# A selective-scan layer on one Trainium2 core: the residual sum put on TensorE, two more scan buffers, and a second pair of every tile multiplied by C on GpSimd

## The chip, the cores and the metric

The kernel runs on one core of one Trainium2 chip. The metric is the device time of one execution in microseconds; the figure of a kernel is the median of its runs. Besides, one execution was taken by the hardware profiler; all views of the profile below come from that one execution, and its own time differs a little from the median.

## What is computed

The program is a stack of four layers on an input x of shape (8, 384, 32, 32), in float32: eight samples, 384 channels, 1024 positions. Each layer normalises x by groups of channels, transforms it and adds the result to x. Layers 0 and 2 are selective state-space ("Mamba") layers, layer 1 is a deformable convolution, layer 3 a displaced depthwise filter. The change touches layer 0 alone. Cut to what matters, layer 0 is:

```python
xz = xseq @ in_proj_w.T                       # 384 -> 2 x 768
xin, z = jnp.split(xz, 2, axis=-1)
u = silu(causal_conv3(xin) + conv_b)
dbc = u @ x_proj_w.T                          # 768 -> 24 + 16 + 16
dt, Bm, Cm = split(dbc)
dt = softplus(dt @ dt_proj_w.T + dt_proj_b)   # per channel and token
def step(h, inp):                             # h: 768 channels x 16 states
    dA = jnp.exp(dt_t[..., None] * A)
    h = dA * h + (dt_t * u_t)[..., None] * B_t[:, None, :]
    y = jnp.einsum('bdn,bn->bd', h, C_t)
    return (h, y)
y = ys + u * D
y = y * silu(z)
x = x + y @ out_proj_w.T                      # the layer's residual sum
```

## The kernel before

**Tiling.** A sample's 1024 tokens are cut into two halves of 512, called steps here: 16 steps in layer 0, a first half (`h == 0`) and a second half (`h == 1`) for each sample. The 768 inner channels are six tiles of 128 partitions (`j`, 0 to 5). The 16 states are taken two at a time, so that each tile has eight pairs (`m`, 0 to 7). One pair of one tile of one step is a unit: 48 units in a step, 768 in layer 0. A unit's data are 128 x 1024 numbers (two states, 512 tokens each).

**A unit** goes through five engines:
- ScalarE (ACT): `decays` (L437) makes exp(dt A) in PSUM, two instructions. There are two such PSUM buffers (`da`).
- GpSimd (POOL): `inputs` (L442) makes the product with B in `db` (three buffers).
- VectorE (DVE): `scan` (L452) runs the recurrence. Normally it writes over `da`.
- Then the states are multiplied by C (`with_c`): normally on VectorE (L466), from `da` into an `hs` buffer in SBUF, 128 x 1024. For the pairs that the table `GP_C` names, the scan writes an `hs` buffer itself and GpSimd multiplies it in place (L463)[...]. There are four `hs` buffers (L450, L465), handed out in the order of the units.
- TensorE (PE): `read_out` (L473 to L486) adds the two states' columns of `hs` into the PSUM tile `y` by products with the identity (L483); the first read of a tile is preceded by the product of u with the diagonal of D (L479).

When all eight pairs of a tile are read, `close` (L503, VectorE) multiplies `y` with the gate and writes it into `u`. There is one `y` buffer, so the next tile's first product (L479) comes after this close.

**Who multiplies with C in layer 0.** `GP_C[0]` holds, by half and by whether the tile's number is even or odd, the pairs for GpSimd: pairs 0 and 4 in every tile of first halves and in even tiles of second halves, pair 0 alone in odd tiles of second halves.

**The order of the work.** Every engine executes its instructions in the order in which the loop at L704 emits them; the order is written out by hand (`manual_schedule`). In unit t of a step (t = 8 j + m) the loop emits: the reads that are due "early"; the ScalarE items planned for t; the scan and, on VectorE, its `with_c`; the decays of the unit two ahead; the VectorE items for t; the GpSimd product with B for the unit three ahead and, where it is GpSimd's, `with_c`; the GpSimd items; the PE items; and the reads that are due "late". A pair that VectorE multiplied is read late, one unit after its own (the last pair of a tile early in the unit after), a pair of GpSimd's early, three units after its own (L744, L745).

**What is planned beside the scans** (`plan`, L591 to L661). A step carries along the end of the step before it and the front of the step after it. The items that matter here, for layer 0:
- `close` of tile j - 1 in unit 8 j + 1, so the close of tile 1 is in unit 17.
- Of the step before: `residual` (L506) in unit 9 reloads x from DRAM into a two-buffer ring; `out_proj` (L516) for the three output groups o on PE in units 8 and 9, 10 and 11, 12 and 13; `out_take` (L536) on VectorE in units 10, 12 and 14, which adds the PSUM result to x in place and, after the third, stores x with one DMA.
- Of this step: `z_proj` (L492, for tile 1 in unit 9), `dt_proj` (L389, for tile 3 in unit 14), and on ScalarE `soft_exp` (L395 to L398, from unit 15).
- Of the step after: `inner` (L333) on PE in units 15, 16, 17, 24, 25 and 26, followed on ScalarE by `conv_last` (L337) and on VectorE by `conv` (L353) one and two units later; `x_proj` (L369) in units 30 and 31. If it is a first half, the group statistics also fall in units 0 to 8.

After the last unit (L748 to L760) the last step's close, residual load, `out_proj` and `out_take` run alone, and then the next layer begins.

All float32 products on TensorE appear in the profile as two matmul instructions each.

Of the kernel before, what the change touches and what calls it, by code (L numbers as in the profile page):

```python
# [8 lines left out]
F32 = mybir.dt.float32  # L9
AF = mybir.ActivationFunctionType  # L10
ALU = mybir.AluOpType
# [4 lines left out]
P = 128  # L16
# [6 lines left out]
ND = DI // P  # L23
# [3 lines left out]
TS = L // 2  # L27
W_MID = 1536


GP_C = {0: (((0, 4), (0, 4)), ((0, 4), (0,))), 2: (((0,), (0,)), ((0,), (0,)))}
GP_ADD = {0: (), 2: (1, 2, 3, 5, 6)}
ENGINES = {mybir.EngineType.Activation, mybir.EngineType.PE, mybir.EngineType.DVE, mybir.EngineType.Pool}
FF = 4 * C
# [57 lines left out]
class Net:  # L92
# [107 lines left out]
    def ssm_layer(self, li, src, dst, shift=None):  # L200
        tc, nc, ins = self.tc, self.nc, self.ins
        mlp = li == 2
        gp_c, gp_add = GP_C[li], GP_ADD[li]
        with ExitStack() as ctx:
            wp = ctx.enter_context(tc.tile_pool(name=f"w{li}", bufs=1))
            p1 = ctx.enter_context(tc.tile_pool(name=f"p1_{li}", bufs=1))
            p2 = ctx.enter_context(tc.tile_pool(name=f"p2_{li}", bufs=2))
# [5 lines left out]
            for h in (1, 0):  # L213
                x = p2.tile([P, G, TS], F32, name="x", tag="x")
# [44 lines left out]
            def w_mid(src, k):  # L259
                t = p2.tile([P, k, W_MID // k], F32, name="wm", tag="wm", bufs=3)  # L260
                n = src.shape[2]
                nc.sync.dma_start(out=t[:, :, :n], in_=src)
                return t
# [180 lines left out]
            def scan(s, j, m):  # L444
                if j == 0 and m == 0 and s["h"] == 0:
                    s["sib"]["st"] = p2.tile([P, ND, NS], F32, name="st")
                da, db = s["da", m], s["db", m]
                h = da
                if m in gp_c[s["h"]][j % 2]:
                    h = s["hs", m] = p2.tile([P, 2, TS], F32, name="hs", tag="hs", bufs=4)  # L450
                h1, da1, db1 = (t.rearrange("p i l -> p (i l)") for t in (h, da, db))
                nc.vector.tensor_tensor_scan(h1, da1, db1, 0.0, ALU.mult, ALU.add)  # L452
                s["h", m] = h
# [6 lines left out]
            def with_c(s, j, m):  # L460
                c = s["bc"][m][:, 1]
                if m in gp_c[s["h"]][j % 2]:
                    nc.gpsimd.tensor_tensor(s["hs", m], s["hs", m], c, ALU.mult)  # L463
                else:
                    hs = s["hs", m] = p2.tile([P, 2, TS], F32, name="hs", tag="hs", bufs=4)  # L465
                    nc.vector.tensor_tensor(hs, s["da", m], c, ALU.mult)  # L466

            def add_pair(s, j, m):
# [41 lines left out]
            def out_proj(s, o, k0, k1):  # L510
                if k0 == 0:
                    wo = w_mid(wout_d[:, :, o * P : (o + 1) * P], ND) if mlp else wout[:, :, o * P : (o + 1) * P]
                    s["out", o] = self.psum("ps_o"), wo
                ps, wo = s["out", o]
                for k in range(k0, k1):
                    nc.tensor.matmul(ps, wo[:, k, :P], s["u"][:, k, :], start=(k == 0), stop=(k == ND - 1))  # L516

            def store(s, o):
                if mlp:
# [9 lines left out]
            def out_take(s, o):  # L529
                if mlp:  # L530
                    if o == 0:
                        s["t"] = p2.tile([P, G, TS], F32, name="t", tag="xn", bufs=3)
                    nc.scalar.copy(s["t"][:, o, :], s["out", o][0])
                else:
                    xo = s["x"][:, o, :]
                    nc.vector.tensor_tensor(xo, xo, s["out", o][0], ALU.add)  # L536
                    store(s, o)

            def mlp_up(s, q, f):
# [51 lines left out]
            def plan(prev, s, nxt):  # L591
                act, dve, pool, pe = queues = [[[] for _ in range(T + NU)] for _ in range(4)]

                def put(q, t, fn, *args):
                    if not args or args[0]:
                        q[t].append((fn, *args))

                for j in range(ND):
                    t = NU * j
                    put(dve, t + 1, close, *((s, j - 1) if j else (prev, ND - 1)))  # L600
                    put(pe, (0, 9, 18, 27, 33, 41)[j], z_proj, s, j)
                    g = (3, 11, 20, 29, 35, 44)[j]
                    put(act, g, gate, s, j)
                    if j in (2, 3):
                        put(act, g, silu, nxt, 3 * (j - 2), 3 * (j - 1))
                    put(act, g, exp_ln)

                    n, k = (s, j + 2) if j + 2 < ND else (nxt, j + 2 - ND)
                    put(pe, t + 6, dt_proj, n, k)
                    put(act, t + 7, soft_exp, n, k)  # L610
                    put(dve, t + 8, soft_rest, n, k)
                    put(act, t + 9, soft_ln, n, k)
                    put(pool, t + 10, soft_sum, n, k)
                put(pe, 0, norm_load, nxt)
                if nxt and nxt["h"] == 0:
                    put(dve, 2, norm_stats, nxt, 0)
                    put(dve, 3, norm_stats, nxt, 1)
                    put(dve, 3, lambda n: n.update(gn_mv=self.gn_aggr(n["gn_st"])), nxt)
                    put(pe, 4, lambda n: n.update(gn_ps=self.gn_mean(n["gn_mv"])), nxt)
                    put(dve, 5, lambda n: n.update(gn_grp=self.gn_dev(n["gn_mv"], n["gn_ps"])), nxt)  # L620
                    put(act, 6, lambda n: n.update(gn_dm=self.gn_square(n["gn_grp"][1])), nxt)
                    put(pe, 6, lambda n: n.update(gn_ps=self.gn_mean2(n["gn_dm"])), nxt)
                    put(dve, 7, lambda n: n.update(gn_var=self.gn_sum(n["gn_grp"][0], n["gn_ps"])), nxt)
                    put(act, 8, lambda n: n.update(gn=self.gn_rstd(n["gn_grp"][0], n["gn_var"])), nxt)
                    put(act, 8, lambda n: n["sib"].update(gn=n["gn"]), nxt)
                put(act, 9, norm_apply, nxt)
                if mlp:
                    put(pe, 10, ln_mean, nxt)
                    put(dve, 11, ln_center, nxt)
                    put(act, 12, ln_square, nxt)  # L630
                    put(pe, 12, ln_var, nxt)
                    put(act, 13, ln_rstd, nxt)
                    put(dve, 13, ln_scale, nxt)
                    put(act, 14, ln_affine, nxt)
                for d, t in enumerate((15, 16, 17, 24, 25, 26)):
                    put(pe, t, inner, nxt, d)
                    put(act, t + 1, conv_last, nxt, d)
                    put(dve, t + 2, conv, nxt, d)
                put(pe, 30, x_proj, nxt, 0, ND // 2)
                put(pe, 31, x_proj, nxt, ND // 2, ND)  # L640
                put(act, 32, x_store, nxt)
                for m in range(NU):
                    put(pool, 41 + m, load_bc, nxt, m)
                put(act, 7 if mlp else 9, residual, prev)
                for o, (t, e) in enumerate(((1, 2), (3, 4), (5, 6)) if mlp else ((8, 9), (10, 11), (12, 13))):
                    put(pe, t, out_proj, prev, o, 0, ND // 2)
                    put(pe, e, out_proj, prev, o, ND // 2, ND)
                    put(act if mlp else dve, e + (1 if mlp else 2), out_take, prev, o)
                if mlp:
                    ups = ((7, 8, 11, 13), (22, 23, 28, 29), (37, 38, 39, 40))  # L650
                    downs = ((19, 20, 21), (34, 35, 36), (43, 44, 45))
                    for q, g in enumerate((17, 33, 42)):
                        for f, t in enumerate(ups[q]):
                            put(pe, t, mlp_up, prev, q, f)
                            put(act, t + 1, up_take, prev, q, f)
                        put(act, g, gelu, prev)
                        put(act, g, exp_ln)
                        for o, t in enumerate(downs[q]):
                            put(pe, t, mlp_down, prev, q, o)
                            put(dve, t + 2, down_take, prev, q, o)  # L660
                return queues  # L661
# [6 lines left out]
            with tc.manual_schedule(engines=ENGINES):  # L668
                s = steps[0]
# [34 lines left out]
                for i, (s, j, m) in enumerate(units):  # L704
                    c, t = divmod(i, T)
                    if t == 0:
# [6 lines left out]
                        act, dve, pool, pe = queues  # L713
# [6 lines left out]
                    if not mine:  # L720
                        with_c(s, j, m)
# [14 lines left out]
                    if mine:  # L736
                        with_c(s, j, m)
# [6 lines left out]
                    k = 3 if mine else 2 if m in gp_add else 1  # L744
# [12 lines left out]
                    stats = list(range(last))  # L757
                for o in range(G):
                    out_proj(s, o, 0, ND)
                    out_take(s, o)  # L760
                if mlp:
                    kernels_a()
# [1084 lines left out]
```

## Time and profile before

| what | value |
|---|---|
| median of three runs | 9474.54 us (9471.22 to 9475.02) |
| the profiled execution's own time | 9480.32 us |
| its span, first to last instruction | 9478.5 us |
| mean granted TensorE clock | 0.948 |
| busy share of the span | PE 90%, DVE 86%, ACT 68%, POOL 61% |
| closes of layer 0 (L503, 96 of them) | start at 97.5 us to 3022.4 us |
| L452, scans of the whole program | 2912.7 + 602.4 us on DVE |
| L442, products with B | 3611.1 us on POOL |
| L483, reads with the identity | 2605.0 us on PE |

How to read it. Times are counted from the first instruction. "PE" are matmuls, "PEld" the loads of their stationary operand, which overlap with them. The matmuls' ends are modelled, so a matmul of 592 ns by the profile may be followed by the next one before it ends; the distance from start to start tells the rate. A busy share of the whole span mixes four layers; layer 0 takes about the first third, and only its stretches matter here. In the tables by windows, each row is a stretch "from:to" with its length, and then the busy time of each engine in it with the number of its instructions, the granted clock, and the DMA share. In the tables of waits, a row is "engine line waited for whom: total us, times, longest us". In timelines, "[1.22 <-PE y L483]" says that the engine sat idle for 1.22 us before this instruction and that the PE's instruction of L483 ended the wait.

### The profile page before, as it was taken

The page shows a single profiled execution, that of the slowest core. Times are in us where ns is not written, and L with a number is a line of the kernel's source. Part 1 is how long each engine was busy: PE and PEld are TensorE (multiplying, and loading weights), DVE is VectorE, ACT ScalarE, POOL GpSimd, SP SyncE. Part 2 cuts the span into 40 slices and gives each one's busy share as a digit, 9 for nine tenths or more (in the row PEclk, how much of TensorE's full clock was granted, in tenths as well). Part 3 has the DMA queues.
Part 4 walks back from the last instruction along what each step waited for, and adds up shares of the span by engine and source line. Part 5 has one row for each costly group of instructions (what it writes and reads, how often), then busy time and mean ns, then how long its engine had stood idle before and what let it go on. Part 6 is the DMA issues. An engine that isn't in the chain of part 4 may idle for free. (4 is left out here: it accounts for less than half of the span.)

```text
span 9478.5 us, 87409 instructions
## 1 busy us (share of the span) xinstructions
PE 8496.4 (90%) x27916; PEld 4511.6 (48%) x27916; DVE 8121.2 (86%) x8881; ACT 6479.3 (68%) x10147; POOL 5774.0 (61%) x3801
## 2 busy tenths in 40 slices
PE   7898888889887899999999997699999999999987
PEld 3333333333333677677777776244343443434333
DVE  7999999999997678778778777899999999999973
ACT  6666666666664677778778777667777777777750
POOL 7888888888887000000000000899999999999974
PEclk8999999999998999999999998799999999999998
DMA  2111211121111233333333333233232433333336
GB/s 92 68 56 46 85 53 53 50 85 56 49 68 51 77 80 88 90 83 84 93 79 88 89 83 87 92 100 95 91 94 87 121 112 96 93 91 90 120 102 127
DMA packets 566065, 791.98 MB, mean 84 GB/s; under 512 B 244243, under 2 KB 397235, under 8 KB 542041
## 3 DMA queue, kind: packets, MB, share of 16 engines
q1 hardware_dynamic: 503492, 775.85, 27.9%
q10 hardware_dynamic: 62100, 10.44, 0.7%
q8 instruction: 223, 3.65, 0.2%
q14 instruction: 250, 2.04, 0.1%
HBM read 716.49 MB, written 69.66 MB: 83 GB/s over the span
## 5 line engine op out<-in xcount | busy, mean ns | idle before, releaser
L442 POOL TENSOR_TENSOR db<-du,bc 128x1024 f32<-128x1024 f32 x1536 | 3611.1, 2356 | 419.0 <-DVE hs L452 230.7
L452 DVE TENSOR_TENSOR_SCAN da<-da,db 128x1024 f32<-128x1024 f32 x1272 | 2912.7, 2290 | 199.4 <-ACT da L437 145.4
L483 PE MATMUL y<-hs,ident 128*128 128x512 f32 x5184 | 2605.0, 638 | 376.2 <-DVE hs L466 233.8
L437 ACT ACTIVATE da<-dt,na 128x512 f32<-128x512 f32 x3072 | 2120.0, 691 | 911.1 <-DVE hs L466 679.9
L410 POOL TENSOR_TENSOR dt<-dt,sp_e 128x512 f32<-128x512 f32 x192 | 244.2, 1272 | 2932.1 <-DVE sp_e L402 2932.1
L483 PEld LDWEIGHTS y<-hs,ident 128*128 128x128 f32 x5184 | 1018.0, 203 | 1863.2 <-issue 1125.3
L1515 PE MATMUL wacc<-fsm,fxk 128*128 128x221 f32 (+34 forms) x10624 | 1657.1, 315 | 98.1 <-DVE fsm L1485 95.5
L1515 PEld LDWEIGHTS wacc<-fsm,fxk 128*128 128x128 f32 x10624 | 1570.1, 195 | 236.5 <-DVE fsm L1485 159.5
L466 DVE TENSOR_TENSOR hs<-da,bc 128x1024 f32<-128x1024 f32 x1272 | 1557.7, 1225 | 115.5 <-PE y L483 12.1
L1485 DVE TENSOR_TENSOR fsm<-fhy,fhx 128x170 f32<-128x170 f32 (+42 forms) x3216 | 1170.8, 428 | 346.2 <-PE wacc L1515 319.3
L1445 ACT ACTIVATE fhy<-fpyx,cell 128x416 f32<-128x416 f32 (+9 forms) x1280 | 645.5, 576 | 388.7 <-DVE fsm L1485 388.7
L1468 DVE TENSOR_TENSOR fxk<-fxt,fwk 128x1024 f32<-128x1024 f32 (+1 forms) x688 | 787.2, 1180 | 10.3 <-ACT fxt L1247 10.3
L452 DVE TENSOR_TENSOR_SCAN hs<-da,db 128x1024 f32<-128x1024 f32 x264 | 602.4, 2282 | 70.4 <-POOL db L430 29.4
L463 POOL TENSOR_TENSOR hs<-hs,bc 128x1024 f32<-128x1024 f32 x264 | 622.3, 2357 | 35.8 <-ACT st L458 35.3
L470 POOL TENSOR_TENSOR hs<-hs 128x512 f32<-128x512 f32 x480 | 609.5, 1270 | 3.5 <-DVE hs L466 3.5
L566 PE MATMUL ps_m<-hid,wm 128*128 128x512 f32 x1152 | 535.9, 610 | 29.7 <-ACT hid L559 24.2
L544 PE MATMUL ps_h<-t,wm 128*128 128x512 f32 x1152 | 539.1, 606 | 16.0 <-DVE x L573 15.8
L1450 ACT ACTIVATE fhy<-fhy,cols 128x1344 f32<-128x1344 f32 (+10 forms) x368 | 530.7, 1442 | 12.0
L458 ACT COPY st<-da 128x2 f32<-128x2 f32 x624 | 97.9, 157 | 505.4 <-DVE hs L466 503.9
L1156 PE MATMUL ps_off<-fxn,fow 128*98 128x465 f32 (+10 forms) x896 | 386.6, 579 | 0.0
L1432 ACT ACTIVATE fhx<-fpyx,cell 128x544 f32<-128x544 f32 (+8 forms) x640 | 380.0, 666 | 0.0
L566 PEld LDWEIGHTS ps_m<-hid,wm 128*128 128x128 f32 x1152 | 220.5, 194 | 329.8 <-issue 261.4
(203 smaller groups left out, 9870.2 us busy)
## 6 DMA issues: line engine op xcount, KB each, us to landing
bc<-bcd SPq DMA_DIRECT2D x256, 1024.0 KB
fpyx<-fposd SPq DMA_DIRECT2D x640, 256.0 KB
wm<-in_w SPq DMA_DIRECT2D x96, 768.0 KB
x<-x SPq DMA_DIRECT2D x71, 768.0 KB
winr<-in_win SPq DMA_DIRECT2D x192, 192.0 KB
x<-in_x SPq DMA_DIRECT2D x40, 768.0 KB
fpyx<-fposd SPq DMA_DIRECT2D x24, 1024.0 KB
wm<-in_wout SPq DMA_DIRECT2D x48, 384.0 KB
```

The source lines that it names most:

```text
L437: nc.scalar.activation(da[:, i, :], s["dt", j], AF.Exp, scale=na[:, j, n : n + 1])
L442: nc.gpsimd.tensor_tensor(db, du, s["bc"][m][:, 0], ALU.mult)
L452: nc.vector.tensor_tensor_scan(h1, da1, db1, 0.0, ALU.mult, ALU.add)
L463: nc.gpsimd.tensor_tensor(s["hs", m], s["hs", m], c, ALU.mult)
L466: nc.vector.tensor_tensor(hs, s["da", m], c, ALU.mult)
L470: nc.gpsimd.tensor_tensor(hs[:, 0, :], hs[:, 0, :], hs[:, 1, :], ALU.add)
L483: nc.tensor.matmul(s["y"], self.ident, s["hs", m][:, i, :], start=first and i == 0, stop=k == NU - 1 and i == n - 1,)
L566: nc.tensor.matmul(ps, s["w2"][:, f, o * P : (o + 1) * P], s["hid", q][:, f, :], start=(f == 0), stop=(f == 3))
L1445: nc.scalar.activation(hy[:, at : at + (yb - ya) * W], pyx[:, 0, ya * W : yb * W], AF.Abs, bias=bias)
L1468: nc.vector.tensor_tensor(t[:, :n], x, wk[:, j : j + 1, :].to_broadcast([P, n, P]), ALU.mult)
L1485: nc.vector.tensor_tensor(self.sub(sm, at, [(r * w, n), (w, r), (1, w)]), self.sub(hy, hy_at[by] + xa, [(r * W, n), (W, r), (1, w)]), self ...
L1515: nc.tensor.matmul(a[:, ya - 4 * o : yb - 4 * o, xa:xb], k, self.sub(sm, sm_at[by], [(w, yb - ya), (1, w)]), start=False, stop=False,)
```

## The change

Three edits, in layer 0 alone (layer 2 keeps its four `hs` buffers, its table row and its path through `out_take`):

1. The ring of `hs` has six buffers instead of four.
2. The residual sum moves. After `out_proj` of a group, PE multiplies x by the identity into the same PSUM tile (`add_residual`), which closes the accumulation. `out_take` becomes a plain copy from PSUM to x on ScalarE. `add_residual` is planned for units 10, 12 and 14 on PE (the o-th one ahead of the next group's `out_proj` there), the copy for units 11, 13 and 15 on ScalarE. At the end of the layer the same is done three times.
3. In odd tiles of second halves GpSimd multiplies pair 4 with C as well: its scan writes `hs`, VectorE's product goes, GpSimd's comes, and the read moves from one unit to three units after the pair's own.

```diff
-GP_C = {0: (((0, 4), (0, 4)), ((0, 4), (0,))), 2: (((0,), (0,)), ((0,), (0,)))}
+GP_C = {0: (((0, 4), (0, 4)), ((0, 4), (0, 4))), 2: (((0,), (0,)), ((0,), (0,)))}
...
+        nhs = 4 if mlp else 6
...
-                    h = s["hs", m] = p2.tile([P, 2, TS], F32, name="hs", tag="hs", bufs=4)
+                    h = s["hs", m] = p2.tile([P, 2, TS], F32, name="hs", tag="hs", bufs=nhs)
...
-                    hs = s["hs", m] = p2.tile([P, 2, TS], F32, name="hs", tag="hs", bufs=4)
+                    hs = s["hs", m] = p2.tile([P, 2, TS], F32, name="hs", tag="hs", bufs=nhs)
...
-                    nc.tensor.matmul(ps, wo[:, k, :P], s["u"][:, k, :], start=(k == 0), stop=(k == ND - 1))
+                    nc.tensor.matmul(ps, wo[:, k, :P], s["u"][:, k, :], start=(k == 0), stop=mlp and k == ND - 1)
+
+            def add_residual(s, o):
+                nc.tensor.matmul(s["out", o][0], self.ident, s["x"][:, o, :], start=False, stop=True)
...
-                    xo = s["x"][:, o, :]
-                    nc.vector.tensor_tensor(xo, xo, s["out", o][0], ALU.add)
+                    nc.scalar.copy(s["x"][:, o, :], s["out", o][0])
                     store(s, o)
...
-                    put(act if mlp else dve, e + (1 if mlp else 2), out_take, prev, o)
+                    if not mlp:
+                        put(pe, e + 1, add_residual, prev, o)
+                    put(act, e + (1 if mlp else 2), out_take, prev, o)
...
                 for o in range(G):
                     out_proj(s, o, 0, ND)
+                    if not mlp:
+                        add_residual(s, o)
                     out_take(s, o)
```

## The prediction, made before the changed kernel was run

> **What bounds the kernel now.** The change touches layer 0 only, so I read its stretch alone. I took the waits of VectorE first, then VectorE's timeline to find the closes (L503), then the busy time between closes, one row for each tile. The waits of VectorE in layer 0:
>
> ```profile
> engine line waited for: us in total, times, longest us
> DVE da L452 <- ACT da L437: 75.3, 82, 1.5
> DVE hs L452 <- PE y L483: 26.3, 21, 3.4
> DVE hs L452 <- POOL db L430: 15.0, 10, 1.6
> ...
> DVE hs L466 <- PE y L483: 12.1, 8, 2.2
> DVE u L503 <- PE y L483: 10.9, 14, 1.2
> ...
> DVE x L536 <- PE ps_o L516: 3.2, 7, 0.5
> ```
>
> VectorE waits little in all. But a close waits for PE 14 times, and 14 is the number of steps that have a step before and one after. The stretches from close to close, of a first half (row one, tile 1) and of the second half after it (tiles 1, 3 and 5):
>
> ```profile
> core 0: us, PE busy (x) PEld busy (x) DVE busy (x) ACT busy (x) POOL busy (x), PEclk, DMA share, GB/s
> ...
> 840.97:872.20 31.23, 31.23 (x73) 13.51 (x72) 28.21 (x20) 20.00 (x38) 25.72 (x13) 1.00 0.22 76
> ```
>
> ```profile
> 1027.19:1062.87 35.68, 35.68 (x84) 15.50 (x83) 29.64 (x21) 18.42 (x29) 28.98 (x23) 1.00 0.19 66
> ...
> 1094.33:1126.62 32.29, 30.43 (x69) 11.37 (x67) 31.60 (x24) 20.85 (x32) 26.48 (x22) 1.00 0.01 2
> ...
> 1155.56:1183.51 27.95, 22.02 (x42) 8.43 (x42) 27.38 (x18) 17.31 (x26) 25.90 (x17) 0.89 0.85 300
> ```
>
> In **tile 1** PE is busy for the whole stretch, in both halves (31.23 of 31.23 us, 35.68 of 35.68), and VectorE has 3.0 and 6.0 us to spare. There lies `out_proj`, 36 matmuls on top of a tile's usual ones. In tiles 3 and 5 VectorE is the full one (31.60 of 32.29, 27.38 of 27.95). So layer 0 has two bounds in turn: PE from about unit 8 to the close of tile 1 in unit 17, VectorE elsewhere. The closes show the handover:
>
> ```profile
> 872.20 0.69 DVE L503 TENSOR_TENSOR u<-y,sz 128x512 f32<-128x512 f32 x1 [1.22 <-PE y L483]
> ```
>
> ```profile
> 1061.32 1.23 DVE L466 TENSOR_TENSOR hs<-da,bc 128x1024 f32<-128x1024 f32 x1
> 1062.87 0.69 DVE L503 TENSOR_TENSOR u<-y,sz 128x512 f32<-128x512 f32 x1 [0.33 <-PE y L483]
> ```
>
> The close of tile 3, at 1126.62, has no wait. PE's timeline shows why:
>
> ```profile
> 1118.71 3.72 PE L483 MATMUL y<-hs,ident 128*128 128x512 f32 x8
> 1122.27 2.74 PE L492 MATMUL ps_z<-xn,win 128*128 128x512 f32 x6
> 1127.36 1.16 PE L479 MATMUL y<-u,diag_d 128*128 128x512 f32 x1 [2.35 <-DVE u L503]
> ```
>
> Its last reads of that tile end at 1122.43, 4.2 us before the close, and it stands idle for 2.35 us until the close frees `y`. So PE has some 4 us of slack at tile 3 and none at tile 1.
>
> **What a matmul costs.** Loads and matmuls alternate one for one, and under a full PE the loads start 0.43 us apart (1050.27, then 1050.70):
>
> ```profile
> 1050.27 0.19 PEld L516 LDWEIGHTS ps_o<-u,wout 128*128 128x128 f32 x1 [0.24 <-issue]
> 1050.70 0.19 PEld L516 LDWEIGHTS ps_o<-u,wout 128*128 128x128 f32 x1 [0.24 <-issue]
> ```
>
> A float32 product is two such instructions, 0.86 us. Check: 72 x 0.43 = 31.0 us, of 31.23 in the first half's tile 1.
>
> [...] The trace has 2355 against 1225 ns for the product with C.
>
> **The change, part by part.** Durations in layer 0:
>
> ```profile
> L466 DVE TENSOR_TENSOR hs<-da,bc 128x1024 f32<-128x1024 f32 x600 | 734.8, 1225 | 59.3 <-PE y L483 12.1 <-DVE da L452 0.5
> L463 POOL TENSOR_TENSOR hs<-hs,bc 128x1024 f32<-128x1024 f32 x168 | 395.7, 2355 | 15.2 <-ACT st L458 15.2
> ...
> L536 DVE TENSOR_TENSOR x<-x,ps_o 128x512 f32<-128x512 f32 x48 | 32.6, 679 | 16.5 <-PE ps_o L516 16.5
> ```
>
> *Residual off VectorE.* 48 x 0.679 = 32.6 us go. In the loop they lie in units 10, 12 and 14, inside the PE-bound stretch, where VectorE waits anyway: worth nothing.
>
> *Residual onto PE.* Three products a step, 6 x 0.43 = 2.57 us, in units 10, 12 and 14: inside the full stretch, ahead of the close of tile 1. Nothing hides it. The 14 steps with a wait at that close pay 14 x 2.57 = 36.0 us. Step 0 has no residual. The last step has no `inner` for a successor in unit 15 (one product of three parts, 2.57 us less), so it pays at most about 0.4.
>
> *Copies on ScalarE.* PSUM to SBUF, 128 x 512: the like copy of L1247 takes 586 ns; 1.8 us a step, ScalarE is busy 20 of 31 us there. But the copy waits for PE in order, and the decays of two units ahead stand behind it. The worst is the third: `soft_exp` of unit 15 already waits 5.24 us for PE at 1054.95. With two residuals ahead, PE reaches it 1.7 us later, the copy adds 0.6, so the scan of unit 17 starts near 1061.3 instead of 1058.92; with its product (3.6 us) VectorE is ready to close at about 1065.0. PE is ready at 1062.87 + 2.57 = 1065.4. So the copies hide, by 0.4 us; if the cover fails they cost up to 1 us in each of 14 steps. The reload of x was due for VectorE at unit 10 and showed no wait; PE gets to it no earlier. The store follows the copy, 2 us later, with nobody waiting in the loop.
>
> *Six buffers.* The ring's waits are 26.3 + 12.1 = 38.4 us. In the timeline they stand at units 8 to 16, ahead of the PE-bound close. Without them VectorE arrives earlier and waits at L503 instead. I take 0; bounds 0 and, if they all counted, -38.
>
> *GpSimd's 24 pairs* (8 second halves x 3 odd tiles): VectorE loses 1.225 us each, 29.4 in all, POOL gains 2.36 each. Tile 1's third of it is PE-bound: 0. In tile 3 PE has 4 us of slack and VectorE none: up to 1.2, less some 0.2 because ScalarE's gate of unit 29 holds the decays of unit 31; I take 1.0. In tile 5 POOL runs without a gap from about unit 36 into the next step, and ScalarE's gate falls on the same unit 44; POOL's lead there is about 3.9 us and shrinks by 1.2 + 2.4 = 3.6. I take 0.8. Together 8 x 1.8 = 14.4 us, bounds 0 and 8 x 2.45 = 19.6.
>
> *End of the layer.* The last step's three groups run alone: PE 15.61 us for 36 matmuls, then 0.69 us of VectorE, then the store that the next layer waits for. Six matmuls more, a copy of 0.59 for an addition of 0.69: +2.5 us.
>
> **Sum:** 36.0 + 0.4 + 2.5 - 14.4 = +24.5 us. The profiled execution would go from 9480.3 to 9504.8; it lies 5.8 above the median of the runs, which therefore goes from 9474.5 to **9499.0** (+0.26%). What is late next at tile 1 is PE itself.
>
> **Rivals.** *A, as forecast*: PE pays, tiles 3 and 5 give a part back. With the bounds of GpSimd's gain, +19 to +39: 9494 to 9513. Chance 0.53. *B, GpSimd's relief is lost as well*: POOL's lead in tile 5 breaks, or the copies hold back the decays by 0.5 to 1 us a step: +39 to +50, 9513 to 9525. For it: POOL's gapless stretch and the thin 0.4 us. Chance 0.11. *C, faster*: VectorE is the bound throughout, and its freed time counts: 32.6 + 29.4 + 38.4 = 100 us, 9374; by half, 9424. It decides if PE has over 2.57 us of room before the close of tile 1. For it: VectorE's 86% to 98% in every row; against it: the rows with PE at 100%. Chance 0.14. *D, nearly no change*: PE starts its full stretch earlier, since VectorE no longer stops in unit 8 of second halves (1 to 3 us each); 8 x 1.5 = 12 us less than A: +12, 9487. Against it: PE, not VectorE, is late there. Chance 0.22.
>
> A measurement of this kernel can tell about 0.2% (19 us) from no change. A and B end above it, C below, D within: slower 0.64, same 0.22, faster 0.14. The range takes in A and most of D and a little of B; C and the far side of B are left out.
>
> **What would show it.** In the profile after: PE busy for all of tile 1's stretch, 33.8 and 38.2 us long; VectorE's wait at L503 grown well over 10.9 us, the waits at L452 and L466 for PE gone; second halves' tiles 3 and 5 shorter by about 1 us. I am wrong if PE has gaps in tile 1, or if that stretch grows by much less than 2.57 us.

## The result, and the profile after

The changed kernel takes 9499.65 us (median of 10 runs, 9498.05 to 9510.53) against 9474.08 us (10 runs beside them): a ratio of 1.0029, 95% interval 1.0019 to 1.0038, slower by 25.6 us. The forecast was 9499.0, slower by 24.5. The profiled execution took 9499.88 us, with a span of 9498.1.

The rows from close to close, as before (tile 1 of a first half; then, in the second half after it, tiles 3 and 5 and, last, tile 1; columns: stretch, its length, then PE, PEld, VectorE, ScalarE, GpSimd busy, the granted clock, DMA):

```profile
839.26:873.16 33.90, 33.90 (x79) 14.70 (x79) 26.53 (x18) 21.37 (x41) 25.98 (x13) 1.00 0.21 71
...
1099.66:1130.53 30.87, 30.22 (x69) 11.55 (x67) 30.35 (x23) 20.85 (x32) 28.70 (x23) 1.00 0.01 3
1159.44:1186.62 27.18, 22.86 (x42) 9.05 (x42) 26.23 (x18) 17.24 (x26) 26.71 (x18) 0.81 0.74 253
1029.19:1068.20 39.01, 39.01 (x91) 16.95 (x90) 26.63 (x16) 18.33 (x29) 30.14 (x24) 1.00 0.16 59
```

TensorE still fills all of tile 1, which is longer by 2.67 us in the first half (31.23 to 33.90) and by 3.33 in the second (35.68 to 39.01). Tile 3 lost 1.42 us (32.29 to 30.87) and tile 5 lost 0.77 (27.95 to 27.18). VectorE's busy time in tile 1 fell by 1.7 us (28.21 to 26.53) and 3.0 us (29.64 to 26.63), and it became waiting (waits of VectorE in layer 0):

```profile
DVE da L453 <- ACT da L438: 144.9, 119, 4.7
DVE u L504 <- PE y L484: 41.4, 20, 2.4
DVE sp_e L403 <- ACT sp_w L399: 33.1, 15, 2.7
DVE hs L453 <- POOL db L431: 19.7, 12, 2.5
```

The waits for a free `hs` buffer (L452 and L466 for PE, 38.4 us before) are gone. In their place stand the wait at the close (10.9 before, 41.4 now) and two chains that hang on PE through ScalarE, which waits 82.6 us for `ps_o` and 56.1 us for `ps_dt`: the decays (75.3, now 144.9) and the softplus (8.9, now 33.1). At the close of tile 1 VectorE had its last product done at 1065.79 and waited for PE:

```profile
1064.56 1.23 DVE L467 TENSOR_TENSOR hs<-da,bc 128x1024 f32<-128x1024 f32 x1
1068.20 0.69 DVE L504 TENSOR_TENSOR u<-y,sz 128x512 f32<-128x512 f32 x1 [2.42 <-PE y L484]
```

At the end of the layer, from the last close to the first instruction that waits for the stored x, it went from 19.74 us (3022.44 to 3042.18) to 22.21 us (3044.90 to 3067.11). That instruction, before and after:

```profile
3042.18 0.10 POOL L960 MEMSET fob<- 128x1 f32 x1 [31.05 <-DMA x<-x]
3067.11 0.10 POOL L967 MEMSET fob<- 128x1 f32 x1 [30.93 <-DMA x<-x]
```

That instant moved by 24.9 us, nearly as much as the medians' 25.6: in the two profiled executions the loss lies in layer 0. The rest of the program, which has the same code, took 5.3 us less in this one execution than in the one before.

### The profile page after: what moved, and what is told of

The parts are those of the page before. It is cut to its first block, busy times and chain, and to the rows that moved or that the text cites. A ratio compares the mean times of both kernels' runs of the same rounds, so it can differ in the third digit from the quotient of the medians.

```text
span 9498.1 us, 87491 instructions
## 1 busy us (share of the span) xinstructions
PE 8531.6 (90%) x28012; PEld 4538.4 (48%) x28012; DVE 8064.3 (85%) x8809; ACT 6498.5 (68%) x10195; POOL 5824.4 (61%) x3825
## 5 line engine op out<-in xcount | busy, mean ns | idle before, releaser
L453 DVE TENSOR_TENSOR_SCAN da<-da,db 128x1024 f32<-128x1024 f32 x1248 | 2857.6, 2290 | 265.7 <-ACT da L438 215.6
L467 DVE TENSOR_TENSOR hs<-da,bc 128x1024 f32<-128x1024 f32 x1248 | 1528.5, 1225 | 95.1 <-DVE da L453 2.3
L464 POOL TENSOR_TENSOR hs<-hs,bc 128x1024 f32<-128x1024 f32 x288 | 678.4, 2356 | 67.9 <-ACT st L459 67.7
L453 DVE TENSOR_TENSOR_SCAN hs<-da,db 128x1024 f32<-128x1024 f32 x288 | 656.7, 2280 | 48.6 <-POOL db L431 33.9
L569 PE MATMUL ps_m<-hid,wm 128*128 128x512 f32 x1152 | 536.5, 611 | 30.3 <-ACT hid L562 25.6
```

The lines of the kernel that those rows point to most:

```text
L569: nc.tensor.matmul(ps, s["w2"][:, f, o * P : (o + 1) * P], s["hid", q][:, f, :], start=(f == 0), stop=(f == 3))
```

## The experiments

The theory (A): in tile 1 TensorE is full, so its work ahead of that tile's close costs its own time there and nothing elsewhere, and VectorE's time counts only in the other tiles. The main rival (C): VectorE is the bound throughout. Eleven kernels; each difference is that of the medians against the kernel before, run beside it, and the brackets have the ratio and its 95% interval. The diffs show the main lines; where a part of the change is left out or put back, its lines in the plan and at the layer's end go with it.

**One part of the change at a time.** First the residual alone, on the kernel before:

```diff
-                    xo = s["x"][:, o, :]
-                    nc.vector.tensor_tensor(xo, xo, s["out", o][0], ALU.add)
+                    nc.scalar.copy(s["x"][:, o, :], s["out", o][0])
...
+                        put(pe, e + 1, add_residual, prev, o)
```

> The kernel before with the residual moved to TensorE and the copy to ScalarE, and nothing else. Theory A (TensorE is full in tile 1): 14 x 2.57 us in the loop, 0.4 in the last step and 2.5 at the layer's end, +39 us, about 9513. Four buffers instead of six make no difference to that. Rival C (VectorE is the bound throughout): its 48 additions of 0.679 us count, -33 us, about 9441.

Measured 9527.68, +53.8 us (ratio 1.0057, 1.0043 to 1.0070). C is out. But it is 15 us more than A's 39. Tile 1 of a first half is as A has it (33.82 us, +2.6); in the profile the surplus lies in second halves, and it is taken up below.

The second pair alone:

```diff
-GP_C = {0: (((0, 4), (0, 4)), ((0, 4), (0,))), ...
+GP_C = {0: (((0, 4), (0, 4)), ((0, 4), (0, 4))), ...
```

> The kernel before with pair 4 of odd tiles of second halves on GpSimd, four buffers. Theory A: nothing in tile 1, about 1.0 us in tile 3 and 0.8 us in tile 5 of each second half, -14 us, about 9460. Rival C: 24 x 1.225 us, -29 us, about 9445. If four buffers are too few for the later read of pair 4, the gain is under 8 us.

Measured 9469.29, -4.6 us (0.9996, 0.9988 to 1.0004): not to be told from none. Four buffers are not the reason, as the fourth kernel shows. Here too the tiles do what A says; tiles 3 and 5 of the second half that starts after 960 us:

```profile
1089.83:1120.77 30.94, 30.22 (x69) 11.53 (x67) 30.35 (x23) 20.85 (x32) 28.70 (x23) 1.00 0.01 2
1149.71:1176.89 27.18, 20.98 (x42) 8.06 (x42) 26.23 (x18) 17.23 (x26) 26.71 (x18) 0.94 0.73 252
```

They are shorter by 1.35 and 0.77 us, as in the changed kernel, and something else gives a part back. In the profile it is tiles 0 and 1: together they are longer than before by 0.6 us on average in second halves and by 0.5 in first halves.

The six buffers alone (the second of the two lines that make an `hs` likewise):

```diff
+        nhs = 4 if mlp else 6
...
-                    h = s["hs", m] = p2.tile([P, 2, TS], F32, name="hs", tag="hs", bufs=4)
+                    h = s["hs", m] = p2.tile([P, 2, TS], F32, name="hs", tag="hs", bufs=nhs)
```

> The kernel before with six hs buffers in layer 0 and nothing else. Theory A: the waits for a buffer become waits at the close of tile 1, and the time stays, 0 to -5 us (the profile after suggests that step 1 alone may win 4 us), about 9472. Rival C: the 38 us of waits for a buffer count, about 9436.

Measured 9469.70, -4.2 us (0.9996, 0.9987 to 1.0004): the time is as A has it. VectorE's waits in layer 0 show what became of the 38.4 us:

```profile
DVE da L453 <- ACT da L438: 95.2, 96, 1.5
DVE x L537 <- PE ps_o L517: 18.8, 14, 1.8
DVE sp_e L403 <- ACT sp_w L399: 17.7, 8, 2.5
...
DVE u L504 <- PE y L484: 14.7, 20, 2.0
```

The wait for a buffer is gone; those for PE's `out_proj` (3.2 before), for the softplus (8.9), for the close (10.9) and for the decays (75.3) have together grown by 48 us. Only 3.8 of that stand at the closes, where A put all of it; the decays have 19.9, `out_proj` 15.6 and the softplus 8.8.

Buffers and pair together, the residual on VectorE; against the changed kernel:

```diff
-                nc.tensor.matmul(s["out", o][0], self.ident, s["x"][:, o, :], start=False, stop=True)
...
-                    nc.scalar.copy(s["x"][:, o, :], s["out", o][0])
+                    xo = s["x"][:, o, :]
+                    nc.vector.tensor_tensor(xo, xo, s["out", o][0], ALU.add)
```

> The changed kernel with the residual back on VectorE: six buffers and the second pair on GpSimd. Theory A: the loss of 39 us goes and the gain of tiles 3 and 5 stays, -14 to -19 us against before, about 9458, so faster than both. Rival B (GpSimd's relief is lost to the GpSimd queue): no gain, about 9474. Rival C: 100 us less what the residual frees, -68 us, about 9406.

Measured 9466.27, -7.6 us (0.9991, 0.9983 to 0.9999): faster than both kernels, by half of what A said. Last, buffers and residual without the pair; against the changed kernel:

```diff
-GP_C = {0: (((0, 4), (0, 4)), ((0, 4), (0, 4))), ...
+GP_C = {0: (((0, 4), (0, 4)), ((0, 4), (0,))), ...
```

> The changed kernel without the second pair: six buffers and the residual on TensorE only. By the prediction's own term the pair is worth 14.4 us in the changed kernel, so this one would be at 9514. By the runs so far (the pair gave 4.6 us with four buffers and 3.4 us with six, since the stretch of slow matmuls before tile 1 took the rest back) it would be at 9503. [...]anything between the two and no closer.

Measured 9525.09, +50.4 us (1.0053, 1.0039 to 1.0067), so that the pair is worth 25.4 us in the changed kernel. I had expected it between 9503 and 9514; it lies outside.

**The place of TensorE's work.** Three products of zeros a step, added to y, once in tile 4 (`j == 4`, shown) and in another kernel in tile 1 (`j == 1`), on the kernel before (`zw` is a tile of zeros):

```diff
+                if not mlp and j == 4 and m in (1, 2, 3):
+                    nc.tensor.matmul(s["y"], zw, s["hs", m][:, 0, :], start=False, stop=False)
```

> The kernel before with three products more a step on TensorE that add zeros (zero weights, hs as the moving side) to y in tile 4: the same added work as the three residual products, 2.57 us a step, in a tile where TensorE has about 5 us of slack before the close. Theory A: no change, within 3 us of 9474. A theory in which TensorE is the bound everywhere: +41 us, 9515.

> The same three products of zeros in tile 1, nothing moved to ScalarE or from VectorE. Theory A: 14 x 2.57 us and under 1 us in the first and the last step, +36 to +41 us, about 9511. If the copies on ScalarE are what costs time in the changed kernel: no change, 9474.

In tile 4: 9471.74, -1.7 us (0.9999, 0.9991 to 1.0007). In tile 1: 9517.94, +44.6 us (1.0046, 1.0033 to 1.0060). The same instructions are free in one place and cost at least their time (16 x 2.57 = 41 us) in the other; the 3.5 us above that are within the interval. Tile 4 of a first half before and with them, then tile 1 of a first half in the other kernel:

```profile
936.99:966.65 29.66, 21.38 (x42) 8.56 (x42) 26.32 (x17) 18.18 (x33) 26.97 (x14) 0.88 0.00 1
933.75:963.06 29.31, 21.69 (x48) 8.70 (x48) 26.33 (x17) 18.18 (x33) 26.98 (x14) 1.00 0.00 1
```

```profile
850.46:884.27 33.81, 33.81 (x79) 14.68 (x78) 28.28 (x20) 20.07 (x38) 25.74 (x13) 1.00 0.21 71
```

Tile 4 has six matmuls more (48 for 42) in a stretch that is no longer than before. TensorE's busy time grew by 0.31 us only, while its granted clock went from 0.88 to 1.00. And 33.81 us with no copy on ScalarE is the 33.82 of the residual alone: the copies cost nothing there.

**One product moved behind the close.** On the changed kernel:

```diff
-                for d, t in enumerate((15, 16, 17, 24, 25, 26)):
+                for d, t in enumerate((16, 17, 18, 24, 25, 26) if not mlp else (15, 16, 17, 24, 25, 26)):
...
-                    g = (3, 11, 20, 29, 35, 44)[j]
+                    g = (3, 11, 20 if mlp else 21, 29, 35, 44)[j]
```

> The changed kernel with the first three input products of the step after planned for units 16, 17 and 18 instead of 15, 16 and 17 in layer 0, and what follows on them one unit later (the gate and silu of unit 20 in unit 21). One product of 2.57 us then comes after the close of tile 1 instead of ahead of it. Theory A: the stretch of tile 1 gets shorter by 2.57 us in the 14 inner steps, and TensorE's 4 us of slack in tile 2 take the product: -36 us against the changed kernel, about 9464. Rival: what follows the product on ScalarE and VectorE, one unit later, gives new waits of the same size in tile 2, and nothing is won, about 9500.

Measured 9462.90 (0.9988, 0.9981 to 0.9994), 36.8 us less than the changed kernel, where A has 36. Tile 1 is at 31.38 us in the first half and 36.51 in the second:

```profile
831.07:862.45 31.38, 31.38 (x73) 13.54 (x72) 26.45 (x18) 19.98 (x37) 28.01 (x14) 1.00 0.17 52
1015.97:1052.48 36.51, 36.51 (x85) 15.82 (x84) 26.55 (x17) 19.44 (x30) 30.78 (x24) 1.00 0.13 44
```

Between the two profiled executions layer 0 is shorter by more than the medians say, 46 us: 34 in tile 1 over 14 steps, as A has it, and 10 in tile 0 of second halves, which A does not name. So the mechanism of A is shown, and a part of the close agreement is luck.

The same move (the diff above) on the kernel with six buffers, the pair, and the residual on VectorE:

> Six buffers, the second pair on GpSimd, the residual on VectorE, and the first three input products one unit later as in the run before this one. Theory A: -14 for the pairs and up to -36 for the shorter stretch of tile 1, but there VectorE has only 3 us (first halves) to 6 us to spare and other waits come next, so -30 to -50 us, 9424 to 9444. Rival: no gain from the move, about 9458.

Measured 9431.97, -41.4 us (0.9956, 0.9942 to 0.9969), better than both kernels.

**Why the parts don't add up.** With and without the pair, the difference is -4.6, -3.4 and -25.4 us in three surroundings; the residual costs 53.8 (alone), 55.4 (with six buffers) and 33.4 us (with buffers and pair); the buffers give 2.6 to 4.2 us in the three surroundings tried. So pair and residual act on something in common. It is the stretch from the last close of a first half to the close of tile 1 in the second half: tile 0 with the group means (`gn_mean`, `gn_mean2` on PE), and tile 1. Two such stretches of the changed kernel, then two of the kernel without the pair:

```profile
995.74:1068.20 72.46, 68.89 (x163) 33.52 (x164) 57.03 (x45) 40.47 (x66) 60.06 (x47) 0.86 0.13 44
1372.21:1442.39 70.18, 67.31 (x163) 31.41 (x164) 56.92 (x46) 40.27 (x66) 60.08 (x47) 0.88 0.14 45
```

```profile
1006.93:1079.53 72.60, 69.15 (x163) 33.47 (x164) 58.17 (x47) 40.54 (x66) 57.16 (x45) 0.86 0.12 36
1385.80:1458.40 72.60, 69.15 (x163) 33.47 (x164) 58.16 (x46) 40.55 (x66) 57.17 (x45) 0.86 0.11 35
```

The same 163 matmuls take 72.46 us at a mean granted clock of 0.86 and 70.18 at 0.88. In the first stretch TensorE waits 2.84 us for the statistics, until 1007.16; its clock is at half from 1006.50, and it stays so until 1023.56, 16.4 us after the work is there again (the end of the wait, then the window at half rate):

```profile
1007.16 3.97 PE L140 MATMUL gn_ps<-gn_mv,gmat 128*128 128x2 f32 x18 [2.84 <-DVE gn_mv L132]
```

```profile
1006.50:1023.56 17.06, 16.40 (x46) 10.84 (x47) 16.17 (x16) 9.93 (x22) 14.11 (x13) 0.50 0.00 1
```

For 17.06 us, 16.40 of them busy, the clock is 0.50. Cut into 100 equal pieces each, the seven such stretches of the changed kernel have a clock of 1.00 or 0.50 in 667 of the 700 pieces, and those of the kernel before in 670; the others stand where it goes from one to the other. So the part at half rate can be read off a row as length x (1 - clock) / 0.5: 20.3 us of 72.46, 16.8 of 70.18. Over all seven such stretches the means are 68.0 us before, 70.9 changed, 72.7 with the residual alone, 72.6 with buffers and residual, 68.6 with the pair alone; of these, 16.4, 17.4, 21.0, 20.5 and 17.5 us are at half rate. So of the 25.4 us that the pair is worth in the changed kernel, by the profiles about 12 are tiles 3 and 5, and about 12 are seven stretches that went from 72.6 to 70.9 us.

That is still a correlation, so the idle time was filled: on the changed kernel, five products of zeros in tile 0 of second halves, three of them just ahead of the group means, 4.3 us of added work in each of seven steps (the expectation counts eight, but the last second half has no step after it and gets none). `fill` multiplies zero weights with `xn`, n times, and adds that to y.

```diff
+                if not mlp and nxt and nxt["h"] == 0:
+                    for t, n in ((3, 1), (4, 3), (6, 1)):
+                        put(pe, t, fill, s, n)
```

> The changed kernel with five products of zeros more in tile 0 of each second half (one in unit 3, three in unit 4 ahead of the group means' products, one in unit 6), added to y, where TensorE stands idle and its clock is then granted at half rate for some microseconds. Clock theory: in second halves the stretch from the close of the tile before to the close of tile 1 holds 2 to 4 us of slow matmuls[...], and this is where a part of the second pair's gain and of the first runs' sums went; with the idle filled, the stretch shrinks from 70 to 72 us to 66 to 69 us in spite of 4.3 us more work, so 15 to 40 us less than the changed kernel, 9460 to 9485. Rival: work on a full TensorE costs its time, 8 x 4.3 = +34 us, about 9534.

Measured 9490.55 (21 runs, 9483.84 to 9495.82, all below the 10 of the changed kernel), 9.1 us less with 30 us more of work on TensorE (10.0 less, if each kernel is taken against the kernel before that ran beside it). The rival is out; the gain is below the 15 that I gave as least. Two of its stretches:

```profile
995.31:1065.73 70.42, 69.68 (x173) 32.60 (x174) 56.93 (x45) 40.28 (x66) 60.17 (x47) 0.91 0.14 45
1369.90:1438.41 68.51, 66.83 (x173) 31.05 (x174) 56.83 (x46) 40.27 (x66) 60.08 (x47) 0.95 0.14 47
```

There are ten matmuls more, and these stretches are about 2 us shorter; over all seven the mean goes from 70.9 to 69.6 us, and the time at half rate from 17.4 to 10.6.

The half rate does not always follow a wait, though. Two windows of this kernel that follow each other, in the first of these stretches:

```profile
1001.82:1015.48 13.66, 13.66 (x54) 7.41 (x52) 13.52 (x15) 6.91 (x12) 11.79 (x9) 1.00 0.19 58
1015.48:1022.30 6.82, 6.82 (x15) 3.72 (x15) 6.79 (x6) 5.93 (x13) 6.46 (x8) 0.50 0.00 0
```

TensorE was busy without a gap for 13.66 us, and the clock still went to 0.50. In those microseconds lie 30 of the 36 matmuls of the group means, of one or two columns each. So these matmuls are a rival to the waits as the cause; no run here tells the two apart.

And the same filling (the diff above) on the fastest version so far:

> The same filling on the fastest version so far (six buffers, second pair, residual on VectorE, first input products a unit later, 9432). Clock theory: its stretches hold 5.8 us of slow matmuls from the group means on; 10 to 25 us less, 9407 to 9422. Rival: the added work costs its time, about 9466, or VectorE is the bound there by now, no change.

Measured 9426.04 (9416.29 to 9427.80, all below the 9429.67 to 9436.33 without the filling), 5.9 us less (7.5 against the kernels before that ran beside them), again the right sign and a smaller size. The 5.8 us of slow matmuls was my estimate; by the profiles, the stretch at 979.26 of the kernel without the filling takes 64.82 us at a mean clock of 0.89, and the one at 975.10 with it 65.37 us at 0.92. The version with it is the fastest kernel of the study, 48.9 us under the kernel before (0.9943, 0.9930 to 0.9957).

## Why the prediction was right, point by point

- **The bound.** Shown: tile 1 is TensorE's (zeros in tile 1 against zeros in tile 4; one product moved behind the close), tiles 3 and 5 of second halves are VectorE's (the pair), and in tile 4 TensorE has room. Tile 0 of second halves is neither's alone: there TensorE waits (2.84 us in the stretch above) and is then slow (a clock of 0.50 for 17.06 us). Of the 36 matmuls of `out_proj` six start ahead of tile 1 in the first half (at 835.56, and the close of tile 0 is at 840.97); this changes nothing in the argument.
- **Residual onto PE**, 2.57 us in each of 14 steps: 2.67 us in the first half's tile 1. In second halves tile 1 itself grew by 3.3 us, and the stretch with tile 0 by 2.9 on average (68.0 to 70.9). Right in size here; with the residual alone the same stretch grew by 4.7.
- **Residual off VectorE**, worth nothing: right; its time became waits. With the products of zeros, where VectorE keeps the additions, tile 1 is as long (33.81 us against 33.82). The additions stood in units 11, 13 and 15, one later than the text ahead of the result has it: `out_take` is planned two units after e = 9, 11 and 13. They lie inside the full stretch all the same.
- **Copies on ScalarE**, hidden by 0.4 us: right that they hide, and the margin is wider. VectorE was ready 2.41 us ahead of the close. I had named the third copy as the worst; the longest wait is at the second, 4.69 us before the scan at 1051.79, which waits for its decays, and it too lies under the full TensorE.
- **Six buffers**, 0: measured -2.6 to -4.2 us, below what the runs can tell. That the waits move and the time stays was right; where they go was not. The forecast has them at L503, the close of tile 1; with the buffers alone, 3.8 of 48 us went there, and the rest to the decays, `out_proj` and the softplus.
- **GpSimd's pair**, 1.0 and 0.8 us in tiles 3 and 5: 1.4 and 0.8. In the last second half tile 3 is 1.2 us longer instead, so all eight together give -14.1 us against the -14.4 forecast. VectorE's waits for GpSimd's `db` grew only from 15.0 to 19.7 us.
- **End of the layer**, +2.5: 22.21 - 19.74 = +2.5.
- **The sum**, +24.5: layer 0 grew by 24.9 in the profile, and the medians differ by 25.6.

What was missing is a term that happened to be small here. The row of tile 0 of the second half had 0.79 in its clock column before the change, and I did not price it:

```profile
995.28:1027.19 31.91, 26.75 (x75) 14.32 (x76) 30.35 (x30) 20.71 (x35) 27.87 (x23) 0.79 0.08 25
```

Along with the time at half rate, the mean stretch differs between kernels with the same work on TensorE by 0.6 to 1.8 us (68.6 against 68.0; 72.7 and 72.6 against 70.9), and seven second halves make up to 13 us of it. For the residual, alone and with buffers, nearly all of the miss (15 us, and 11 beyond the range) is there. For the pair alone (9 us missed) less than half is. And the time at half rate is not the whole account: with six buffers and the residual on VectorE the pair lengthened the mean stretch from 68.3 to 68.9 us, though its time at half rate fell from 18.6 to 17.5. In the changed kernel the mean differs from the one before by 2.9 us where the added work is 2.57, so it nearly cancels. That the median agrees to a microsecond is luck, and so is the size, as far as a term of up to 13 us was left out; the sign is not, since the residual's 36 us less the pair's 14 are more than that, and both were shown.

What stays open: why a kernel settles at one length of the half-rate time (every one of seven stretches at 72.60 us without the pair) or mostly alternates between two (70.2 and 72.5 with it). No run shows the reason. Open, too, is whether the half rate comes from the waits, from the short matmuls of the group means, or from both.

## What to carry to other kernels

Cut the profile at the points where engines must meet (here the closes), and read the fullest engine of each stretch: the same three products cost 44.6 us in one tile and nothing in another, though TensorE's share of the span was 90% in both. Taking work off an engine that waits in that stretch, or giving it more buffers, moved its waits elsewhere here, and won nothing that the runs can tell (two more buffers: -4.2 us, 0.9987 to 1.0004). Before adding up small terms, look at the granted clock of the stretches: here tiles 0 and 1 of second halves had 0.85 to 0.93 together, and the same pair was worth 4.6, 3.4 or 25.4 us in three surroundings.

## What the runs showed that was not expected

Useless matmuls in the place of waits made two kernels faster, by 9.1 and 5.9 us. TensorE's clock had stood at 0.50 for 17.06 us at a time, while it was 16.40 us busy; in the first of the two kernels the time at half rate fell from 17.4 to 10.6 us a stretch. The fastest version, 9426.04 us, keeps the residual on VectorE, has six buffers and the second pair on GpSimd, starts the next step's first products after the close of tile 1, and fills the wait for the group means.
